# Steps two to four of a four-node LSTM: a second, outer seven-product form around the one in use

## The chip, the core and the metric

The kernel runs on one core of a Trainium2 chip. TensorE (PE) multiplies matrices out of SBUF into PSUM; VectorE (DVE) and ScalarE (ACT) empty PSUM and work element by element; GpSimd (POOL) works on SBUF alone; SyncE (SP) issues the DMAs. The metric is the device time of one launch in microseconds, the median of three runs. Everything is 32-bit float.

## The reference

The kernel computes a stack of four pre-normalised graph layers on x of shape (128, 64, 256), with one 64 by 64 adjacency. What matters here is the end of layer 0 and the start of layer 1:

```python
for p in range(1, MAX_SKIP + 1):                 # MAX_SKIP = 4
    nw = Tv // p
    wins = h[:, :nw * p, :].reshape(Bv * nw, p, Hd)
    last = _lstm_last(Wih[p - 1], Whh[p - 1], bih[p - 1], bhh[p - 1], wins)
    idx = jnp.arange(nw) * p + (p - 1)
    h = h.at[:, idx, :].set(last.reshape(Bv, nw, Hd))

# _lstm_last, one step j of p (zero state at j = 0; i, f, g, o each 256 wide):
g = x_t @ Wih.T + h @ Whh.T + bias
c = sigmoid(f) * c + sigmoid(i) * tanh(gg)
h = sigmoid(o) * tanh(c)

# then: x = x + layer0(...); layer 1 starts with
h = relu(layernorm(x))                           # aggregated by A_hat, then h @ W1.T
```

The change touches p = 4 only, its steps j = 1, 2 and 3, and the hand-over from there to layer 1.

## The kernel before

**Layout.** The nodes' features lie in `hT`, transposed: features on the partitions (two chunks of 128, index c), nodes along the columns. `cols(blk, c, p, j)` picks the columns of node j of each window. For p = 4 there are 512 columns per block, and the blocks form two pairs; the kernel calls a pair with its state `st` (pool `lh0` or `lh1`). It takes the pairs in turn: step 0 of both, step 1 of both, and so on, eight steps in all.

**The seven-product form.** A gate's weight is 256 by 256, so two by two blocks of 128; its data are two feature chunks by two column blocks (a pair). Instead of eight block products, Strassen's scheme in Winograd's variant needs seven, of sums of weight blocks (`S1`, `S2`, `S3`, `S4`, made once per weight on POOL by `weight_sum`, L311) and sums of data blocks (`tx` for the inputs, made on DVE at L650; `th` for the state, made on DVE or POOL in `state_sums`). `gate` (L675) issues these: seven products of the input weight (L688), and for j > 0 seven of the hidden weight (L694) into the same banks a, b and c, 512 columns each. ACT copies (L713) and DVE adds (L710) empty the banks into the gate's tile, and ACT applies bias and sigmoid or tanh (L706). A step without state (j = 0) has three gates and 21 products, one with state four gates and 56.

**After the gates.** `step` (L740) multiplies and adds the cell (L733: on POOL, or on DVE where `both` is given `nc.vector`), ACT takes tanh (L738), and `state` (L653) writes h, or in the last step the result into `hT` (L658), on DVE.

**Order.** The order on each engine's queue is written out by hand: every operation is put into a list by `at(t, ...)` with a virtual time and issued in the order of these times. An engine works off its queue in order, so an operation that waits holds back all behind it. Tiles have fixed places; a new tile in a used place waits for the last reader. PSUM has eight banks of 512 columns, in one pool of eight.

**The weights.** `load` (L791) brings the next p's input weights early and the hidden weights at the start of p (four DMAs of 256 KB each on SP's queue); the sums of the hidden weights follow before step 1. `w1`, layer 1's weight, is loaded at the start of the kernel, and its sums are made in the graph stage (s == 12).

**The hand-over.** While the last LSTM steps run, `begin` (L839) puts layer 1's first tiles between them. For a tile: load x (L572), transpose `hT` back (`turn`, L581, on PE), add it to x (`turned` with direct=True, L587, on DVE from PSUM), statistics (L604, L605) on DVE, the root (L611) on POOL, relu (L616) on ACT, aggregation (`agg`, L625, on PE) and its copy (L629, DVE). `ag_sums` (L837) then prepares the first seven-product form of layer 1, whose products are at L932.

## Time and profile before

| | us |
|---|---|
| median of three runs (lowest, highest) | 1866.76 (1866.54, 1866.87) |
| span of the profiled execution | 1864.5 |
| runs' median less that span | 2.3 |
| busy in the span: PE, DVE, ACT, POOL | 1845.1, 1097.8, 943.3, 816.6 |
| p = 4: about 889 us to the last LSTM product | 1217 |
| layer 1's first product (L932) starts | 1216.99 |

Times inside the kernel are those of one profiled execution, counted from its span's start; the runs are timed from outside, so 2.3 us lie around the span. "Busy" is the time in which an engine had an instruction in work; a matmul's end is modelled by the profile, so two neighbours can overlap in the records, and how far apart they start says more than how long each lasts. A group's row gives the line, the engine, what is written from what, the count, and the mean length in ns.

### The profile page before, as it was taken

To read this page: it belongs to the slowest core of one execution; us is meant where nothing else is said; L and a number is where in the kernel's file an instruction comes from. 1 tells how busy PE (TensorE), PEld (TensorE's weight loads), DVE (VectorE), ACT (ScalarE), POOL (GpSimd) and SP (SyncE) were. 2 spreads that over 40 slices of the span, in tenths; PEclk is the share of its full clock that TensorE was granted. 3 is DMA by queue.
4 is the path that set the end of the run, shared out by engine and by line. 5 is a ranking of instruction groups with operands and counts; after the bars stand their busy time and mean duration, and the time that the engine had idled before them with its cause. 6 is when DMAs were issued, how large, how long until landed. Compare 5 with 4: busy or idle time off the path is not lost.

```text
span 1864.5 us, 21317 instructions
## 1 busy us (share of the span) xinstructions
PE 1845.1 (99%) x7668; PEld 1177.0 (63%) x7668; DVE 1097.8 (59%) x2180; ACT 943.3 (51%) x1622; POOL 816.6 (44%) x773
## 2 busy tenths in 40 slices
PE   8999999999999999999999999999999999999999
PEld 7997444444445666666444444566544899999997
DVE  6775777634546434444633333688876666666664
ACT  6776766534535334433633333477675354444442
POOL 4451423443423533422442222267454566666663
PEclk9999999999999999999999999999999999999999
DMA  5110000000001000000000000333110101111111
GB/s 146 58 58 0 1 1 26 19 1 0 1 0 46 1 0 1 1 1 1 23 0 0 0 0 0 102 113 113 47 47 1 46 12 47 46 46 46 46 46 35
DMA packets 51433, 54.96 MB, mean 29 GB/s; under 512 B 3200, under 2 KB 46720, under 8 KB 51328
## 3 DMA queue, kind: packets, MB, share of 16 engines
q1 hardware_dynamic: 50880, 53.30, 9.1%
q8 instruction: 61, 1.00, 0.2%
q14 instruction: 44, 0.36, 0.1%
q10 hardware_dynamic: 448, 0.30, 0.0%
HBM read 36.55 MB, written 17.04 MB: 29 GB/s over the span
## 4 chain that ended last, share of the span: by engine, by line
PE 93%; DVE 3%; POOL 1%; ACT 1%; issue 1%; DMA 1%; SPq 0%; DVEq 0%; POOLq 0%; ACTq 0%
PE ps L688 34%; PE ps L694 19%; PE ps L1322 8%; PE ps L932 5%; PE ps L1049 4%; PE ps L1409 3%; PE ps L394 3%; PE ps L404 3%; PE ps L1289 2%; PE ps L433 2%; PE ps L1385 2%; PE ps L1419 2%; PE ps L1450 1%; PE ps L625 1%; PE ps L1357 1%; PE ps L581 1%
## 5 line engine op out<-in xcount | busy, mean ns | idle before, releaser
L710 DVE TENSOR_TENSOR gate<-gate,ps 128x512 f32<-128x512 f32 (+2 forms) x378 | 224.0, 620 | 449.1 <-PE ps L694 367.7
L688 PE MATMUL ps<-tx,wih 128*128 128x512 f32 (+2 forms) x996 | 441.3, 541 | 1.9 <-ACT gate L713 1.0
L688 PE MATMUL ps<-hT,wih 128*128 128x512 f32 (+2 forms) x756 | 338.6, 541 | 0.0
L713 ACT COPY gate<-ps 128x512 f32<-128x512 f32 (+2 forms) x252 | 134.3, 533 | 378.6 <-PE ps L694 325.5
L688 PEld LDWEIGHTS ps<-tx,wih 128*128 128x128 f32 x996 | 188.4, 190 | 188.2 <-issue 128.2
L706 ACT ACTIVATE gate<-gate,lbias 128x512 f32<-128x512 f32 (+2 forms) x252 | 216.7, 860 | 160.1 <-DVE gate L710 160.1
L694 PE MATMUL ps<-h,whh 128*128 128x512 f32 (+2 forms) x576 | 256.6, 527 | 0.0
L688 PEld LDWEIGHTS ps<-hT,wih 128*128 128x128 f32 x756 | 143.6, 190 | 141.6 <-issue 79.4
L733 POOL TENSOR_TENSOR gate<-gate 128x1024 f32<-128x1024 f32 (+2 forms) x36 | 71.9, 2019 | 297.6 <-ACT gate L706 297.6
L694 PE MATMUL ps<-th,whh 128*128 128x512 f32 (+2 forms) x432 | 192.4, 527 | 0.0
L694 PEld LDWEIGHTS ps<-h,whh 128*128 128x128 f32 x576 | 109.5, 190 | 100.2 <-issue 76.5
L733 POOL TENSOR_TENSOR cell<-gate 128x1024 f32<-128x1024 f32 (+2 forms) x36 | 79.4, 2230 | 174.8 <-ACT gate L706 174.8
L694 PEld LDWEIGHTS ps<-th,whh 128*128 128x128 f32 x432 | 82.1, 190 | 75.1 <-issue 57.4
L1265 ACT ACTIVATE h<-x,ln_rn 128x256 f32<-128x256 f32 x128 | 68.0, 592 | 92.8 <-POOL ln_rn L1262 92.7
L733 POOL TENSOR_TENSOR cell<-gate,cell 128x1024 f32<-128x1024 f32 (+2 forms) x31 | 62.8, 2044 | 110.2 <-ACT gate L706 110.2
L1322 PE MATMUL ps<-wl,ag 128*128 128x128 f32 x900 | 108.4, 276 | 0.6
L1322 PEld LDWEIGHTS ps<-wl,ag 128*128 128x128 f32 x900 | 104.2, 192 | 3.3 <-ACT ag L1294 2.5
L713 DVE COPY gate<-ps 128x512 f32<-128x512 f32 (+2 forms) x126 | 78.6, 624 | 20.8 <-PE ps L694 20.8
L706 ACT ACTIVATE gate<-ps,lbias 128x512 f32<-128x512 f32 (+2 forms) x126 | 79.5, 631 | 3.8 <-PE ps L694 1.0
L738 ACT ACTIVATE gate<-cell 128x1024 f32<-128x1024 f32 (+2 forms) x72 | 68.0, 951 | 26.1 <-POOL cell L733 26.1
L650 DVE TENSOR_TENSOR tx<-hT,tx 128x512 f32<-128x512 f32 (+2 forms) x70 | 57.7, 824 | 13.8 <-PE ps L688 10.2
L733 POOL TENSOR_TENSOR cell<-cell,gate 128x1024 f32<-128x1024 f32 (+2 forms) x31 | 65.5, 2134 | 0.4
(253 smaller groups left out, 3168.2 us busy)
## 6 DMA issues: line engine op xcount, KB each, us to landing
xt<-in_x_dram SPq DMA_DIRECT2D x30, 512.0 KB, 4.3
x1d<-xt SPq DMA_DIRECT2D x16, 512.0 KB, 2.9
x<-x1d SPq DMA_DIRECT2D x16, 512.0 KB, 4.8
out_dram<-x SPq DMA_DIRECT2D x15, 512.0 KB, 3.8
wih<-in_WihT_dram SPq DMA_DIRECT2D x16, 256.0 KB, 4.9
whh<-in_WhhT_dram SPq DMA_DIRECT2D x12, 256.0 KB, 4.9
xt<-in_x_dram SPq DMA_DIRECT2D x6, 128.0 KB, 2.8
wl<-in_W_dram SPq DMA_DIRECT2D x4, 192.0 KB, 4.0
```

The source lines that it names most:

```text
L650: yield nc.vector.tensor_sub(t[k], *((b[1][0], b[0][0]), (b[1][1], t[0]), (b[1][1], b[1][0]), (b[0][1], t[1 % len(t)]))[k])
L688: nc.tensor.matmul(wide(p_[:, :N]), wih[0][:, OF[k], gi, :], x_, start=first_, stop=(j == 0), skip_group_check=True)
L694: nc.tensor.matmul(p_[:, :N], whh[0][:, OF[k], gi, :], h_, start=False, stop=True, skip_group_check=True)
L706: nc.scalar.activation(to, r[bank_][:, :N] if bank_ else to, fn, bias=lbias[:, l, m : m + 1])
L710: nc.vector.tensor_add(slot(n, hc), slot(n, hc), r[bank_][:, :N])
L713: op(slot(n, hc), r[bank_][:, :N])
L733: fn(*((t["G"] if isinstance(t, dict) and "G" in t else st["c"])[:, n, :, : st["N"]] for t in tiles))
L738: nc.scalar.activation(o_, c, AF.Tanh)
L932: nc.tensor.matmul(r[name], con["w1"][:, OF[j], g, :], x_, start=new, stop=(name, j) in (("a", 4), ("b", 3), ("c", 2)), skip_group_check=True)
L1049: nc.tensor.matmul(banks[name], w2[:, OF[j], k, :], x_, start=(new and k == 0), stop=(k == 1), skip_group_check=True)
L1265: nc.scalar.activation(v[tag][:, q, :], v[src][:, q, :], AF.Relu, bias=v["rn"][:, 1, q : q + 1], scale=v["rn"][:, 0, q : q + 1])
L1322: nc.tensor.matmul(v["g", name][:, p_, :], x_[:, m, ts(p_, P)], wl2[:, OF[j], m, :], start=new and p_ == m == 0, stop=m == 2 and (name, j) ...
```

## The change

For p = 4, steps 1 to 3 no longer call `step` but `outer_step`. A step computes all four gates from x and h together, so its product as a whole has again a two by two shape: rows are the gate pairs (i, g) and (o, f), the inner index is x or h, and columns are the pair's two column blocks. An outer seven-product form goes over these, with weights S1 to S4 (`outer_sum`, on POOL, made once from the input and the hidden weights) and data T1 to T4 (T1 and T3 on DVE, T2 and T4 on POOL). Of its seven outer products, four (5, 2, 4, 3) are computed each by the inner seven-product form, per gate, over two halves of 256 columns (`strassen`, whose data sums are made by `inner_sum` on POOL). Three (1, 6, 7) are computed directly, eight block products of 512 columns each, all into the same four banks k0 to k3 (`direct`). `SEQ` mixes the 28 inner products (each for two gates) and the 24 direct ones evenly. `take` empties an inner bank (ACT copy or DVE add), `chained` a direct one after each of the three products.

The four-node weights are stored in the order i, g, o, f (`load_in_order`, with more and smaller DMAs). Tiles are placed by hand to make room (`outer_places`): the place of `w1` holds some of the sums until the end, so `w1` is loaded in the hand-over and its four sums are made there. PSUM is eight single banks with names, which p = 1 to 3 use in turn (`next_bank`). In step 0 of p = 4 the cell's first products of the second pair go to DVE. In the hand-over `turned` is now an ACT copy, `added` (L593 before, on POOL) adds it to x; the first tile's aggregation is copied by ACT; and the virtual times are others. `fin` marks the last step, which orders some operations differently and splits the last cell operations in two.

```diff
+    def load_w1():
...
-            if s in (9, 12):
+            if s == 9:
                 for k in range(4):
-                    at(1.4 + 1.3 * k, lambda k=k: weight_sum(wih0[0] if s == 9 else con["w1"], k))
+                    at(1.4 + 1.3 * k, lambda k=k: weight_sum(wih0[0], k))
...
-        def turned(self, k, direct=False):
-
-            v, qs = self.v, slice(2 * k, 2 * k + 2)
-            if direct:
-                nc.vector.tensor_add(v["xt"][:, qs], v["xt"][:, qs], v["T", k])
-            else:
-                nc.scalar.copy(v["h"][:, qs], v["T", k])
+        def turned(self, k):
+
+            nc.scalar.copy(self.v["h"][:, slice(2 * k, 2 * k + 2)], self.v["T", k])
...
+    PLACES = ("c", "a0", "b", "k0", "k1", "a1", "k2", "k3")
+    new_banks(**{n: 1 for n in PLACES})
+    turn_ = {"bank": 6, "gate": 0, "a": 0}
+
+    def next_bank():
+        turn_["bank"] += 1
+        return bank(("c", "a0", "k0", "k1", "a1", "b", "k2", "k3")[(turn_["bank"] - 1) % 8])
...
+            due = p == NL and st["pool"] is lh1
             for n in range(2):
-                at(e + 0.1 * n, both(nc.gpsimd.tensor_mul, st, "c", g["i"], g["g"]), n)
+                at(e + 0.1 * n + 0.7 * due, both((nc.vector if due else nc.gpsimd).tensor_mul, st, "c", g["i"], g["g"]), n)
             squash, g["t"] = both(tanh_of, st, g["g"], "c"), g["g"]
             ready = e + 3.5 * u, e + 6.0 * u
-            h_at = t + 13.3
+            h_at = t + (11.5 if p == NL and st["pool"] is lh1 else 13.3)
...
+        if not last and p < NL:
...
+    ORDER = (0, 2, 3, 1)
+    outer = {}
+
+    def load_in_order(src, w):
+        v = src.rearrange("(c p) (g h m) -> h c p g m", p=P, g=4, m=P)
+        for h in range(2):
+            for c in range(2):
+                nc.sync.dma_start(w[:, 2 * h + c, 0:2], v[h, c][:, 0:3:2])
+                for to, g in ((2, 3), (3, 1)):
+                    nc.sync.dma_start(w[:, 2 * h + c, to], v[h, c][:, g])
...
+    def outer_sum(name, engine=nc.gpsimd):
+        x, h, s1, s2, s4 = (outer[n] for n in ("wx", "wh", "s1", "s2", "s4"))
+        M1, M2 = slice(0, 2), slice(2, 4)
+        if name == "S1":
+            engine.tensor_add(s1[:, 0:4], x[:, :, M2], h[:, 0:4, M2])
+        elif name == "S2":
+            engine.tensor_sub(s2, s1[:, 0:4], x[:, :, M1])
+        elif name == "S3":
+            engine.tensor_sub(x[:, :, M2], x[:, :, M1], x[:, :, M2])
+        elif name == "S4":
+            engine.tensor_sub(outer["s4raw"], h[:, 0:4, M1], s2)
+        else:
+            of, k = name
+            w = {"S1": [s1[:, m] for m in range(7)], "H": [h[:, m] for m in range(7)], "S4": s4}[of]
+            op = engine.tensor_sub if k else engine.tensor_add
+            op(*(w[m] for m in ((S1, A21, A22), (S2, S1, A11), (S3, A11, A21), (S4, A12, S2))[k]))
...
+    INNER = (("a", 1), ("c", 2), ("a", 6), ("b", 5), ("a", 7), ("b", 3), ("a", 4))
+    SEQ = sorted([((i + 0.25) * 52 / 28, "S", i) for i in range(28)] +
+                 [((k + 0.5) * 52 / 24, "D", k) for k in range(24)])
+    AT = {(kind, i): n for n, (_, kind, i) in enumerate(SEQ)}
+    CHAIN = ((0, 1), (1, 1), (0, 0), (1, 0))
+    FN = {(0, 0): AF.Sigmoid, (0, 1): AF.Tanh, (1, 0): AF.Sigmoid, (1, 1): AF.Sigmoid}
...
+        def data(pr):
+            v = {5: lambda: T("T1")[:, :, :N], 2: lambda: h(0), 4: lambda: T("T4")[:, :, :N], 3: lambda: h(1)}[pr]()
+            return halves(v), [s[:, :H] for s in T({5: "T1s", 2: "h1s", 4: "T4s", 3: "h2s"}[pr])]
+
+        def inner_sum(pr, k, engine=nc.gpsimd):
+            b, s = data(pr)
+            engine.tensor_sub(*((s[0], b[0, 1], b[0, 0]), (s[1], b[1, 1], s[0]),
+                                (b[0, 1], b[1, 1], b[0, 1]), (s[2], b[1, 0], s[1]))[k])
+
+        def strassen(pr, i):
+            name, k = INNER[i]
+            if i == 0:
+                turn_["a"] ^= 1
+            if (name, k) in (("a", 1), ("b", 5), ("c", 2)):
+                B[pr, name] = bank(f"a{turn_['a']}" if name == "a" else name)
+            b, s = data(pr)
+            d = (b[0, 0], b[1, 0], b[1, 1], s[2], s[0], s[1], b[0, 1])[k - 1]
+            m = OF[k]
+            w = {5: lambda: outer["s1"][:, m], 2: lambda: outer["wh"][:, m, 0:2],
+                 4: lambda: outer["wh"][:, m, 2:4], 3: lambda: outer["s4"][m]}[pr]()
+            for g in range(2):
+                nc.tensor.matmul(B[pr, name][:, g * H : (g + 1) * H], w[:, g, :], d,
+                                 start=(g == 0 and (name, k) in (("a", 1), ("b", 5), ("c", 2))),
+                                 stop=(name, k) in (("a", 4), ("b", 3), ("c", 2)), skip_group_check=True)
...
+        def half(pr, hc, d):
+            return tile_of({5: "22", 2: "11", 4: "21", 3: "12"}[pr])[:, :, hc, d * H : (d + 1) * H]
+
+        def take(pr, i):
+            name, k = INNER[i]
+            hc, d = ((0, 0), (0, 0), (0, 1), (1, 1), (1, 1), (0, 1), (1, 0))[i]
+            v = B[pr, name][:, : 2 * H].rearrange("p (g t) -> p g t", g=2)
+            if pr in (5, 4) and i in (0, 2, 3, 6):
+                nc.scalar.copy(half(pr, hc, d), v)
+            else:
+                nc.vector.tensor_add(half(pr, hc, d), half(pr, hc, d), v)
+
+        def direct(pr, k, c):
+            hc, g = CHAIN[k]
+            if pr == 1 and c == 0:
+                B[k] = bank(f"k{k}")
+            m = 2 * hc + c
+            w = {1: lambda: outer["wx"][:, m, g], 6: lambda: outer["s2"][:, m, g],
+                 7: lambda: outer["wx"][:, m, 2 + g]}[pr]()
+            d = x(0, c) if pr == 1 else T({6: "T2", 7: "T3"}[pr])[:, c, :N]
+            to = wide(B[k][:, :N]) if pr == 1 else B[k][:, :N]
+            nc.tensor.matmul(to, w, d, start=(pr == 1 and c == 0), stop=(c == 1), skip_group_check=True)
...
+        def chained(pr, k):
+            v = B[k][:, :N]
+            if pr == 1:
+                nc.scalar.copy(part("11", k), v)
+            elif pr == 6:
+                nc.vector.tensor_add(part("12", k), part("22", k), v)
+            else:
+                for m in ("21", "22"):
+                    nc.vector.tensor_add(part(m, k), part(m, k), v)
...
+        def in_times_g(n, c=slice(0, KC)):
+            m = ("11", "12")[n]
+            nc.gpsimd.tensor_mul(gate_(m, 0)[:, c], gate_(m, 0)[:, c], gate_(m, 1)[:, c])
+
+        def keep(n):
+            nc.gpsimd.tensor_mul(cell(n), cell(n), gate_(("21", "22")[n], 1))
+
+        def plus(n, c=slice(0, KC)):
+            nc.gpsimd.tensor_add(cell(n)[:, c], cell(n)[:, c], gate_(("11", "12")[n], 0)[:, c])
+
...
+            nc.vector.tensor_mul(h(n), gate_(m, 0), gate_(m, 1))
...
+        def T1(c):
+            nc.vector.tensor_sub(wide(T("T1")[:, c, :N]), x(1, c), x(0, c))
+
+        def T2(engine=nc.gpsimd):
+            engine.tensor_sub(T("T2")[:, :, :N], h(1), T("T1")[:, :, :N])
+
+        def T3(c):
...
+            nc.vector.tensor_sub(wide(T("T3")[:, c, :N]), wide(h(1)[:, c]), x(1, c))
+
+        def T4():
+            nc.gpsimd.tensor_sub(T("T4")[:, :, :N], h(0), T("T2")[:, :, :N])
...
+            prep(-38 + 0.6 * c, T1, c, needs_h=False)
+        for k, s in ((0, -35), (1, -34), (3, -33)):
+            prep(s, inner_sum, 5, k, needs_h=False)
+        for k, s in ((0, -25), (1, -24), (3, -23)):
+            prep(s, inner_sum, 2, k)
+        prep(-15, T2)
+        prep(-14.9, inner_sum, 5, 2)
+        late = 8 if one else -11
+        prep(late, T4)
+        prep(late + 0.1, inner_sum, 2, 2)
+        for k in range(4):
+            prep(late + 2 + k, inner_sum, 4, k)
+        late = 18 if fin else 1
+        for c in range(KC):
+            prep(late + 0.6 * c, T3, c)
+        for k in range(4):
+            prep(late + 6 + k, inner_sum, 3, k)
+
+        for n, (_, kind, i) in enumerate(SEQ):
+            if kind == "S":
+                mi, i = divmod(i, 7)
+                tick(n, strassen, (5, 2, 4, 3)[mi], i)
+                tick(n + 1.1, take, (5, 2, 4, 3)[mi], i)
+            else:
+                di, i = divmod(i, 8)
+                tick(n, direct, (1, 6, 7)[di], *divmod(i, 2))
+                if i % 2:
+                    tick(n + 1.15, chained, (1, 6, 7)[di], i // 2)
...
+        e = AT["D", 19] + 4.2
+        for n in range(2):
+            tick(e + 0.2 * n, keep, n)
+        tick(e + 0.1, plus, 0)
+        tick(54.6, squash, 0)
+        for i, (g, hc) in enumerate(((0, 0), (1, 0), (0, 1), (1, 1))):
+            tick((51.3, 53.5)[hc] + 0.1 * g if fin else (58.2, 61.2)[hc] + 1.2 * g, act, "12", g, hc)
+        e = 56.2 if fin else 63
+        for c in range(KC if fin else 1):
+            c = slice(c, c + 1) if fin else slice(0, KC)
+            tick(e, in_times_g, 1, c)
+            tick(e, plus, 1, c)
+        tick(58.5, out, 0)
+        tick(e + 4.2, squash, 1)
+        tick(e + 6, out, 1)
+        st["h_at"] = t0 + 0.5 * (e + 6)
+        return t0 + 26
...
+        elif p > 1:
+            at(t + 7.5, outer_places, l)
+            for when, name in ((16, "S1"), (18.8, "S2"), (21.6, ("S1", 0)), (23.5, ("S1", 1)), (24.5, ("S1", 2)),
+                               (25.5, ("S1", 3)), (27, ("H", 0)), (28.5, ("H", 1)), (30, ("H", 3)),
+                               (48.2, "S4"), (48.3, ("H", 2)), (50, "S3"), (52, ("S4", 0)), (52.5, ("S4", 1)),
+                               (53, ("S4", 2)), (53.5, ("S4", 3))):
+                at(t + when, outer_sum, name)
...
-                    if p == NL and turn:
-                        turn = None if st is sts[-1] else False
+                    if p == NL and j:
+                        if j == 1 and st is sts[0]:
+                            t += 3
+                            n = turn_["gate"] - 1
+                            tags = {"22": (n + 1) % 5, "11": (n + 2) % 5, "12": (n - 2) % 5,
+                                    "21": (n - 1) % 5, "spare": n % 5}
+                        else:
+                            tags = dict(tags)
+                            tags["22"], tags["spare"] = tags["spare"], tags["22"]
+                        t = outer_step(t, st, j, j == p - 1, l, tags, j == p - 1 and st is sts[-1])
+                        continue
                     t = step(t, st, j, j == p - 1, l, wt[l], turn)
...
-    t -= 28
+    t -= 26
+    seam = []
+
+    def seam_bank():
+        if not seam:
+            return bank(f"a{1 - turn_['a']}")
+        seam.append(seam.pop(0))
+        return bank(seam[-1])
...
+        def turned(k):
+            f.turn(k)
+            f.turned(k)
+
+        def added(k):
+            f.added(k)
+            if k:
+                f.store()
+
+        def agg(c):
+            f.agg(c)
+            f.agged(c, nc.vector.tensor_copy if s else nc.scalar.copy)
...
+    at(t + 7.6, make_room)
+    begin(0, 7.7, 11.4, 12.5, 16.3, 23.2)
+    begin(1, 7.8, 16, 17.1, 21.1, 28)
+    begin(2, 7.9, 20.3, 21.4, 25.3)
+    begin(3, 17, 24.3, 25.4)
+    begin(4, 21.4)
+    at(t + 17.3, load_w1)
     for k in range(4):
-        at(t + 35.3 + 0.1 * k, ag_sums, 0, k, nc.vector)
+        at(t + 24 + 0.1 * k, lambda k=k: weight_sum(con["w1"], k))
+    at(t + 26.1, lambda: seam.extend(("a0", "a1", "c", "b")))
+    at(t + 34, lambda: First(3).root())
+    for k in range(4):
+        at(t + 28.7 + 0.1 * k, ag_sums, 0, k, nc.vector)
```

## The prediction

> **What bounds the kernel now.** I read the page's busy table and its chain first.
>
> ```profile
> PE 1845.1 (99%) x7668; PEld 1177.0 (63%) x7668; DVE 1097.8 (59%) x2180; ACT 943.3 (51%) x1622; POOL 816.6 (44%) x773
> ...
> PE 93%; DVE 3%; POOL 1%; ACT 1%; issue 1%; DMA 1%; SPq 0%; DVEq 0%; POOLq 0%; ACTq 0%
> PE ps L688 34%; PE ps L694 19%; PE ps L1322 8%; PE ps L932 5%; PE ps L1049 4%; PE ps L1409 3%; PE ps L394 3%; PE ps L404 3%; PE ps L1289 2%; PE ps L433 2%; PE ps L1385 2%; PE ps L1419 2%; PE ps L1450 1%; PE ps L625 1%; PE ps L1357 1%; PE ps L581 1%
> ```
>
> TensorE (PE) is busy 99% and carries 93% of the chain; the LSTM products (L688, L694) alone are 53% of it. So every product that is removed shortens the kernel, unless an engine that was hidden becomes late. Next, busy time by window (columns: window, its length, then busy time and instructions of PE, weight loads, VectorE (DVE), ScalarE (ACT), GpSimd (POOL), granted clock, DMA share, GB/s): the layer-4 LSTM's stretch, two of its steps, and the hand-over to layer 1.
>
> ```profile
> 921.00:1210.00 289.00, 289.00 (x710) 130.94 (x709) 122.24 (x195) 104.37 (x144) 92.46 (x48) 1.00 0.05 17
> 1105.00:1153.00 48.00, 48.00 (x113) 21.28 (x112) 18.65 (x26) 16.51 (x22) 13.93 (x6) 1.00 0.00 0
> 1153.00:1201.00 48.00, 48.00 (x131) 22.73 (x130) 24.04 (x52) 19.48 (x29) 15.84 (x10) 1.00 0.21 69
> 1201.00:1229.00 28.00, 27.66 (x118) 16.30 (x117) 23.30 (x49) 16.39 (x26) 12.41 (x9) 1.00 0.32 100
> ```
>
> PE never pauses from 921 to 1210 us, at full granted clock, and loses 0.34 us in the hand-over. DVE, ACT and POOL have more than half of each step free. That slack is what the change spends.
>
> **The products.** The timeline on PE, a step of 512-column products and a run of 256-column ones (start, time, line, shape, count):
>
> ```profile
> 1105.09 1.02 PE L688 MATMUL ps<-tx,wih 128*128 128x512 f32 x2
> 1105.95 1.02 PE L694 MATMUL ps<-th,whh 128*128 128x512 f32 x2
> ...
> 69.03 3.62 PE L404 MATMUL ps<-wg,g 128*128 128x256 f32 x16
> ```
>
> A product leaves two records, and the next product starts 0.86 us later (1105.95 − 1105.09), 0.859 as a mean over many. For 256 columns, 16 records take 3.62 us; the last lasts about 0.38 (the group's mean is 380 ns), so they start (3.62 − 0.38)/15 = 0.216 us apart, and a product takes 0.431 us. A step at j = 1, 2 or 3 has 4 gates × 7 × 2 = 56 products, 48.1 us (the 48 us windows hold 113 records). In the changed kernel it has four outer products, each 7 inner ones × 2 gates of 256 columns, 56 × 0.431 = 24.2 us, and three direct ones of 8 products each, 24 × 0.859 = 20.6 us: 44.8 us. Six steps: 6 × (48.1 − 44.8) = **−19.9 us**.
>
> [...]
>
> **What feeds them.** DVE per step: 20 inner adds and 12 chained ones out of PSUM (L710's row: 684 ns), 21.9 us, and T1, T3 and the two outputs, about 5 us: 27 of 44.8. ACT: 12 copies (584 ns), 16 activations (722) and 2 tanh (1,048): 20.7. POOL: 16 sums of 256 columns (L425's row: 729 ns), 11.7 us, and eight 1024-column ones (T2, T4, two each of i·g, keep and plus; 2,351 ns), 18.8: 30.5 of 44.8, where before had 13.9 to 15.8 of 48. None exceeds PE, so load alone costs nothing; order can. Two things bring order in. One is the place where DVE and POOL hold each other up (timeline):
>
> ```profile
> 576.97 1.22 DVE L733 TENSOR_TENSOR cell<-gate,cell 128x1024 f32<-128x1024 f32 x1 [1.70 <-ACT gate L706]
> 578.30 3.19 DVE L733 TENSOR_TENSOR cell<-cell,gate 128x1024 f32<-128x1024 f32 x1
> ...
> 577.79 2.62 POOL L733 TENSOR_TENSOR cell<-gate,cell 128x1024 f32<-128x1024 f32 x1 [7.36 <-ACT gate L706]
> ```
>
> The second DVE instruction, of the same size, starts while POOL runs one, and takes 3.19 instead of 1.22 us. DVE's add out of PSUM at 581.41 keeps to 0.68 while POOL is busy. So T1, T3 and the outputs (two SBUF inputs) can each lose up to one POOL instruction, 2.35 us, and the 32 adds can't. [...]
>
> The other is the queue behind the output. Output 1 waits on DVE for tanh 1 (ACT), which waits for POOL's i·g 1 and plus 1; behind it on DVE stands the add that empties the bank of inner product S2.2, needed again two inner products later. Counting from the order, DVE has only 0.2 to 0.3 us to spare there. Bounds: 0 (a step of before loses nothing) to 2.35 (one POOL instruction); I take 0.3 in five of six steps, **+1.5 us**, nearer to zero because the adds themselves aren't slowed.
>
> **The transition from j = 0.** The weights' outer sums (S1 to S4 of 1024 columns, and twelve inner ones of 256 or 512) now follow on POOL, behind the hidden weights' load (issued at 889, in 12 DMAs instead of 4; landing rows: 4.9 us each) and beside DVE's input differences. Most have more than 5 us of room. Bounds 0 to 5 us (two POOL instructions); I take **+1.0**, near the low end, as 921 to 1210 shows no wait behind the sums made today. SP's queue holds nothing else in that stretch that anyone awaits soon.
>
> **The hand-over to layer 1.** Before, DVE added PSUM to x (L587). Now ACT copies and POOL adds (L593's row: 1,275 ns), the four sums of w1 (4 × 0.73 = 2.9 us; they leave the graph stage, where POOL is busy 4 to 5 tenths and PE 9, so nothing is gained there) lie on POOL here, and its banks are rotated, some reused at once. The row that prices a reuse:
>
> ```profile
> 1213.75 0.69 DVE L629 COPY ag<-ps 128x512 f32<-128x512 f32 x1 [0.20 <-PE ps L625]
> ...
> 1215.09 0.37 PEld L688 LDWEIGHTS ps<-tx,wih 128*128 128x128 f32 x2 [0.49 <-DVE gate L710]
> 1215.27 1.02 PE L688 MATMUL ps<-tx,wih 128*128 128x512 f32 x2
> ```
>
> PE to evictor 0.20, ACT copy 0.58, release to the next product 0.23 (L710 ends at 1215.04): 1.0 us. In the order:
> (i) the third tile's turn is followed directly by S3.0 on the same bank, and the fourth's by the first aggregation: 2 × 1.0, a third place 0.3: 2.3 us.
> (ii) The second tile's aggregation waits for DVE's last inner add, queued behind the fourth tile's statistics, which wait for POOL's add behind keep, plus, keep (3 × 2.35): 1.7 to 2.5.
> (iii) The third tile's aggregation waits for a DVE copy queued behind statistics that wait for POOL's add behind w1's sums (2.9): 1.8 to 2.0.
> (iv) A layer-1 product waits for an ACT eviction behind the last tanh, which waits for POOL's halves of i·g and plus (4 × 1.275): 2.7 to 6.5.
> (ii) and (iii) hold PE back 3.5 us, which (iv)'s chain uses: it keeps 0 to 3.0, taken as 1.5. With the low ends of (ii) and (iii), as these chains start from products further ahead than I can place exactly: 2.3 + 1.7 + 1.8 + 1.5 = **+7.3 us**. Bounds: 0, as in before's hand-over (0.34), and 13.3, all four at their tops.
>
> Layers 1 to 3 and the LSTMs of one to three nodes get the same instructions with the same dependencies (eight single banks take turns where one pool of eight did): 0, between −1 and +1 (PE's idle time there is about 2 us).
>
> **Sum** against the profiled execution: 1864.5 − 19.9 + 1.5 + 1.0 + 7.3 = 1854.4 us of span; 2.3 us lie around the span (median 1866.76), so **1856.7 us**.
>
> **The rivals.** All hidden (0.14): the terms given back stay near zero, as the idle halves of the three engines would have it: 1864.5 − 19.9 + 0 to 3 + 2.3 = 1847 to 1850. Against it stand the direct bank reuses (i), which no slack removes.
> Given back in full (0.10): the hand-over at its top (13.3), the steps at 0.7 each: 1864.5 − 19.9 + 13.3 + 4.2 + 2.5 + 2.3 = 1867: no change. For it: DVE is busy about 45 of 52 us there.
> POOL becomes the bound (0.12), on the slower side: with 30.5 of 44.8 us and a recurrence that passes POOL five times per step (i·g, keep, plus, T2 or T4, inner sums), a late output makes the next step's sums late, so slack isn't regained. It decides from (19.9 − 8.3)/6 = 1.9 us of stall per step; with one and a half POOL instructions (3.5 us) per step the time is 1866.8 + 6 × 3.5 − 19.9 + 8.3 = 1876. Against it: a POOL instruction's whole length, 2.35, would have to show in each step, and POOL has 14 us of idle time to catch up in.
> The smaller products aren't half as long (0.01): were the 56 further loads per step (190 ns each) to lie bare, 6 × 56 × 0.190 = 64 us, 1921 us; L404's row is against it.
> My forecast, part of it given back mainly at the hand-over, has 0.63: 1850.5 to 1863.
>
> A difference of 0.2%, 3.7 us, is about what can be told from no change here. Faster by more: 0.63 + 0.14 + part of the third = 0.78; within: 0.09; slower: 0.13. The range leaves out the lowest few hundredths and POOL's case: 1848 to 1867.
>
> **What would show it.** Right: PE's 256-column records 0.216 us apart, a step of about 45 us, PE waits of 5 to 9 us around the turns (L588), aggregation (L626) and the first layer-1 products (L1265), under 0.5 us per step elsewhere. Wrong: waits of 2 us or more in every step for POOL's or DVE's sums, or no waits at the hand-over at all.

## The result, and the profile after

The changed kernel takes 1864.36 us (median of 20 runs, 1861.67 to 1866.61); the kernel before took 1866.91 beside it (20 runs, 1866.25 to 1867.52). The ratio is 0.9987, with an interval of 0.9980 to 0.9994: faster by 2.5 us, an eighth of the 19.9 us of products that were removed. The forecast was 1856.7, so 7.7 us more came back than was forecast. Two things in the numbers ask for an answer: where the rest went, and why runs of the changed kernel differ by 5 us among themselves where those of before differ by 1.3.

The page after, busy times and chain:

```profile
PE 1832.1 (98%) x7956; PEld 1234.1 (66%) x7956; DVE 1162.3 (62%) x2250; ACT 964.1 (52%) x1680; POOL 949.1 (51%) x895
...
PE 92%; POOL 2%; DVE 2%; ACT 2%; issue 1%; DMA 1%; SPq 0%; POOLq 0%; DVEq 0%; ACTq 0%
```

PE is still the bound, but its busy time fell by 13.0 us only (1845.1 to 1832.1), not 19.9: some of the remaining products got longer. The windows say where. Columns are as in the prediction; the granted clock is the third number from the end. First the transition out of step 0 in the kernel before, which the prediction did not look at by itself:

```profile
898.00:945.00 47.00, 47.00 (x110) 20.72 (x109) 29.42 (x36) 24.89 (x34) 25.39 (x16) 1.00 0.00 0
```

and in the kernel after, that stretch, two whole outer steps, and pieces of the slow stretches:

```profile
898.00:945.00 47.00, 42.19 (x110) 21.57 (x109) 35.47 (x38) 23.40 (x34) 46.45 (x34) 0.93 0.00 0
1005.00:1050.00 45.00, 45.00 (x162) 30.55 (x161) 29.07 (x38) 18.96 (x30) 33.93 (x25) 1.00 0.00 1
1050.00:1095.00 45.00, 45.00 (x162) 30.46 (x161) 29.29 (x39) 18.96 (x30) 33.94 (x25) 1.00 0.00 1
...
912.00:915.00 3.00, 3.00 (x5) 1.23 (x4) 1.98 (x3) 0.72 (x1) 2.92 (x4) 0.50 0.00 0
936.00:939.00 3.00, 2.81 (x5) 1.60 (x6) 0.00 (x0) 1.08 (x2) 3.00 (x3) 0.50 0.00 0
1220.00:1222.00 2.00, 2.00 (x6) 0.97 (x5) 1.16 (x2) 1.64 (x4) 1.92 (x3) 0.50 0.00 0
```

The outer steps themselves run as forecast: PE is busy without a gap, at full clock. In the transition POOL is busy 46.45 of 47 us, PE 42.19, and the granted clock is 0.50 in two places; once more in the hand-over. The timeline on PE, with the waits in brackets, shows what precedes each of the three:

```profile
911.00 2.80 PE L701 MATMUL ps<-tx,wih 128*128 128x512 f32 x4 [2.26 <-ACT gate L726]
936.18 2.07 PE L965 MATMUL ps<-hT,wih 128*128 128x512 f32 x2 [2.54 <-ACT gate L719]
974.83 1.03 PE L940 MATMUL ps<-early 128*128 128x256 f32 x4
1019.60 1.03 PE L940 MATMUL ps<-early 128*128 128x256 f32 x4
1190.58 1.13 PE L940 MATMUL ps<-h,wih 128*128 128x256 f32 x4 [0.68 <-ACT h L588]
1199.30 1.16 PE L626 MATMUL ps<-ahT,h 128*128 128x128 f32 x8 [0.67 <-ACT ag L588]
1207.46 2.05 PE L626 MATMUL ps<-ahT,h 128*128 128x128 f32 x16 [1.25 <-DVE gate L954]
1212.78 1.13 PE L626 MATMUL ps<-ahT,h 128*128 128x128 f32 x8 [1.55 <-DVE ag L630]
1217.93 1.10 PE L1265 MATMUL ps<-T,w 128*128 128x512 f32 x2 [3.16 <-ACT hS L1270]
```

Two waits in the transition, none between 940 and 1190, five in the hand-over. A whole step lasts 1019.60 − 974.83 = 44.77 us. Each of the three longest waits is followed by half the clock: the products from 911.00 to 917.06 are five, 4.3 us at full clock, and took 6.06, which is 1.8 lost; in the same way 1.6 at 936.18 and 1.7 from 1218.87 on. The account for the profiled execution:

| | forecast, us | found, us |
|---|---|---|
| products removed | −19.9 | −19.9 (6 × (48.1 − 44.77) = −20.0) |
| waits in the steps | +1.5 | 0 |
| waits in the transition | +1.0 | 2.26 + 2.54 = +4.8 |
| waits in the hand-over | +7.3 | 0.68 + 0.67 + 1.25 + 1.55 + 3.16 = +7.3 |
| half clock after three waits | none | 1.8 + 1.6 + 1.7 = +5.1 |
| wait of before that is gone | none | −0.3 |
| sum | −10.1 | −3.0 |

The spans differ by 1863.0 − 1864.5 = −1.5. All of that arises in the stretch of the change: ahead of it the two timelines lie 0.05 us apart (the same product starts at 879.73 before and 879.78 after), and from the turn at 1230.77 before and 1229.22 after they keep a distance of 1.5 to 1.6 us to the end, so the LSTMs of one to three nodes and the layers behind the hand-over gave nothing back. Of the 1.5 us left over in the account, restarts are about 0.5 (the first product after a wait takes about 0.95 us to the next instead of 0.86, at five places in the hand-over); the rest isn't resolved.

### The profile page after: what moved, and what is told of

It is laid out like the page before. It is cut to its first block, busy times and chain, and to the rows that moved or that the text cites. A ratio compares the mean times of both kernels' runs of the same rounds, so it can differ in the third digit from the quotient of the medians.

```text
span 1863.0 us, 22263 instructions
## 1 busy us (share of the span) xinstructions
PE 1832.1 (98%) x7956; PEld 1234.1 (66%) x7956; DVE 1162.3 (62%) x2250; ACT 964.1 (52%) x1680; POOL 949.1 (51%) x895
## 4 chain that ended last, share of the span: by engine, by line
PE 92%; POOL 2%; DVE 2%; ACT 2%; issue 1%; DMA 1%; SPq 0%; POOLq 0%; DVEq 0%; ACTq 0%
PE ps L701 26%; PE ps L707 12%; PE ps L1655 8%; PE ps L940 7%; PE ps L965 6%; PE ps L1265 5%; PE ps L1382 4%; PE ps L396 3%; PE ps L406 3%; PE ps L1742 3%; PE ps L1622 2%; PE ps L435 2%; PE ps L1718 2%; PE ps L1752 2%; PE ps L1783 1%; PE ps L626 1%
## 5 line engine op out<-in xcount | busy, mean ns | idle before, releaser
L723 DVE TENSOR_TENSOR gate<-gate,ps 128x512 f32<-128x512 f32 (+2 forms) x306 | 176.6, 604 | 303.1 <-PE ps L707 227.6
L701 PE MATMUL ps<-tx,wih 128*128 128x512 f32 (+2 forms) x804 | 344.2, 530 | 4.2 <-ACT gate L726 3.3
L701 PE MATMUL ps<-hT,wih 128*128 128x512 f32 (+2 forms) x612 | 265.9, 530 | 0.0
L719 ACT ACTIVATE gate<-gate,lbias 128x512 f32<-128x512 f32 (+2 forms) x204 | 171.7, 842 | 117.1 <-DVE gate L723 117.0
L707 PE MATMUL ps<-h,whh 128*128 128x512 f32 (+2 forms) x384 | 158.6, 494 | 0.0
L755 POOL TENSOR_TENSOR gate<-gate 128x1024 f32<-128x1024 f32 (+2 forms) x24 | 43.9, 1851 | 181.8 <-ACT gate L719 181.8
L954 DVE TENSOR_TENSOR gate<-gate,ps 128x512 f32<-128x512 f32 x120 | 82.0, 683 | 69.4 <-PE ps L940 67.0
L707 PE MATMUL ps<-th,whh 128*128 128x512 f32 (+2 forms) x288 | 118.9, 494 | 0.0
L985 ACT ACTIVATE gate<-gate,lbias 128x512 f32<-128x512 f32 x96 | 64.9, 717 | 57.4 <-DVE gate L954 30.3
L755 POOL TENSOR_TENSOR cell<-gate,cell 128x640 f32<-128x640 f32 (+2 forms) x20 | 37.2, 1874 | 67.4 <-ACT gate L719 67.4
L1742 PE MATMUL ps<-wvo,h3T 128*128 128x256 f32 x256 | 65.5, 379 | 0.0
```

Of the source, the lines that this page charges most:

```text
L701: nc.tensor.matmul(wide(p_[:, :N]), wih_of(l, k, gi), x_, start=first_, stop=(j == 0), skip_group_check=True)
L707: nc.tensor.matmul(p_[:, :N], whh[0][:, OF[k], gi, :], h_, start=False, stop=True, skip_group_check=True)
L719: nc.scalar.activation(to, r[bank_][:, :N] if bank_ else to, fn, bias=lbias[:, l, m : m + 1])
L723: nc.vector.tensor_add(slot(n, hc), slot(n, hc), r[bank_][:, :N])
L755: fn(*((t["G"] if isinstance(t, dict) and "G" in t else st["c"])[:, n, :, : st["N"]] for t in tiles))
L954: nc.vector.tensor_add(half(pr, hc, d), half(pr, hc, d), v)
```

## The experiments

All runs change the kernel after, but for the two with pauses, which change the kernel before. Waits are PE's in the profiled execution of each, between 905 and 945 (transition) and 1185 and 1225 (hand-over). The last column is the time lost to half clock there: the granted clock's distance from 1.00, times the window, summed over windows of 0.5 us.

| run | median (range), us | span, us | waits in transition | waits in hand-over | lost to half clock |
|---|---|---|---|---|---|
| kernel after | 1864.36 (1861.67–1866.61) | 1863.0 | 2.26, 2.54 | 7.3 | 5.1 |
| e1_cells_first | 1868.84 (1863.50–1869.54) | 1867.1 | 3.02, 3.25 | as after | 8.5 |
| e2_dma_order | 1864.08 (1861.74–1866.54) | 1863.2 | 1.39, 3.66 | as after | 5.1 |
| e3_t3_late | 1861.46 (1859.54–1862.85) | 1860.5 | 2.51, 1.41 | as after | 3.4 |
| e4_cells_first_t3_late | 1862.18 (1860.89–1862.94) | 1860.6 | 3.01, 1.06 | as after | 3.4 |
| e5_t1_late | 1865.93 (1860.78–1867.23) | 1864.5 | 0.45, 0.86, 3.44 | 7.3 | 6.8 |
| e6_t1_t3_late | 1860.55 (1859.93–1861.58) | 1858.3 | 0.47, 0.82, 1.41 | 7.3 | 1.7 |
| e7_seam | 1862.11 (1861.70–1863.04) | 1860.4 | 2.29, 3.92 | 0.69, 2.71, 1.24 | 3.4 |
| e8_all | 1857.23 (1856.80–1859.41) | 1855.1 | 0.44, 0.84, 1.41 | 0.69, 2.71, 1.24 | 1.7 |
| e11_best | 1856.83 (1856.34–1859.06) | 1856.5 | 0.45, 0.82, 0.42 | 0.69, 2.72, 2.68 | 1.7 |
| e12_pool_load | 1856.73 (1856.36–1857.94) | 1854.6 | 0.45, 0.84, 0.41 | 0.69, 2.69, 1.50 | 1.7 |

The waits and the half clock are nearly all that sets these versions apart: the span less both lies between 1845.0 and 1847.0 us in all eleven, while the spans run from 1854.6 to 1867.1.

**Is POOL late with the cells, or are the weights?** e1_cells_first:

```diff
...
-(16, "S1"), (18.8, "S2"), (21.6, ("S1", 0)), (23.5, ("S1", 1))
+(16, "S1"), (22.5, "S2"), (22.4, ("S1", 0)), (23.5, ("S1", 1))
...
```

> The two cell products of step 0 (L755) go ahead of the second outer weight sum and one inner sum on POOL's queue. Theory (order): the first wait of PE in the transition (2.3 us before 911.0) comes from those sums standing ahead of the cells, which holds up tanh on ACT and behind it the copy that empties a bank; and the halved clock after it (912 to 915.5, about 1.7 us) comes from the pause. Then both go: 1864.4 - 2.3 - 1.7 = 1860.4 us, and the granted clock has one dip less. Rival (load): POOL is busy 47.6 of 48 us from 897 to 945, so what is moved behind is late instead; a wait of about 2 us turns up before 945 and the time stays within 1 us of 1864.4. Rival (loads of weights): the twelve smaller DMAs land too late; the order changes nothing, 1864.4.

My first theory fell. The cells ran first, tanh and the copy were in time, and PE waited longer:

```profile
911.91 2.96 PE L701 MATMUL ps<-tx,wih 128*128 128x512 f32 x4 [3.02 <-DVE tx L662]
```

None of the three times expected was met: the median is 4.5 us above the kernel after. In the profiled executions (1867.1 against 1863.0) the waits are 1.5 us longer and the half clock, which lasted about 6.8 us after two of the three long waits instead of 3.4, costs 3.4 more. The first wait is now put down to DVE's input difference L662. In the kernel after, both ended within 0.15 us of each other, and the profile had named the later one, ACT. The timeline on DVE of the kernel after shows why L662 is late:

```profile
906.02 3.69 DVE L1017 TENSOR_TENSOR early<-hT,hT 128x512 f32<-128x512 f32 x2
909.64 1.22 DVE L662 TENSOR_TENSOR tx<-hT 128x512 f32<-128x512 f32 x1
...
928.28 3.92 DVE L1027 TENSOR_TENSOR T<-h,hT 128x512 f32<-128x512 f32 x2
932.13 0.67 DVE L954 TENSOR_TENSOR gate<-gate,ps 128x512 f32<-128x512 f32 x1
932.73 0.67 DVE L723 TENSOR_TENSOR gate<-gate,ps 128x512 f32<-128x512 f32 x1
```

T1 (L1017) stands ahead of L662, and T3 (L1027) ahead of the last add of step 0 (L723). Both read two SBUF inputs while POOL works without a pause, and take 3.7 and 3.9 us for two instructions (T1 0.93 and 2.84, T3 2.25 and 1.75); the adds out of PSUM beside them keep to 0.67. The same T3 in the last outer step, where POOL runs nothing from 1167.91 to 1173.36, takes 0.69:

```profile
1170.37 0.69 DVE L1027 TENSOR_TENSOR gate<-h,hT 128x512 f32<-128x512 f32 x1
```

That POOL is what stretches them is read from these rows; no run takes POOL's work away from beside T1 and T3. e2_dma_order issues first all the DMAs that the first sum needs:

```diff
-        load_in_order(a["WhhT"][l], outer["wh"])
...
+        for m in range(4):
+            for to, g in ((2, 3), (3, 1)):
+                nc.sync.dma_start(w[:, m, to], v[m // 2, m % 2][:, g])
+        for m in range(4):
+            nc.sync.dma_start(w[:, m, 0:2], v[m // 2, m % 2][:, 0:3:2])
```

> The eight DMAs of the hidden weights that the first outer sum reads are issued first, the four others behind them; nothing else. POOL's first sum started at 897.66, when the last of twelve had landed; it should start about 4 x 0.55 = 2.2 us earlier, at 895.5. Theory (order on POOL): the sums ahead of the cells are then done by 902.0 and the cells start at 902.4 as in the kernel before, so the first wait (2.3) and its slow clock (1.7) go: 1860.4 us. Rival (load): POOL gains 2.2 us, so the wait shrinks but what follows stays saturated: 1862 to 1864. If the dominant cause is DVE and POOL holding each other up rather than POOL's lateness: 1864, the wait stays.

POOL's first sum did start at 895.34 and the cells at 902.61, as expected; yet the first wait only shrank to 1.39, the second grew to 3.66, and the time stayed. So late weights had a share in the first wait, but earlier weights alone buy nothing.

**T3 and T1 behind what a bank waits for.** e3_t3_late, and e5_t1_late:

```diff
-            prep(late + 0.6 * c, T3, c)
+            prep((6 if one else late) + 0.6 * c, T3, c)
```

> In the first outer step T3's two subtractions on DVE (928.28, 3.92 us instead of 1.4) go behind the next inner add and the last add of step 0 (L723). Theory (order, with POOL blocking DVE): the second wait (2.5 us before 936.18) goes, as the add runs at 928.3 instead of 932.7, and with it the slow clock behind it (1.7): 1864.4 - 4.2 = 1860.2 us. Rival (load): another operation waits for POOL's sum in its place, PE still pauses 2 us or more between 930 and 945: 1864. Rival (no clock effect, the records only show it): 1861.9.

```diff
-            prep(-38 + 0.6 * c, T1, c, needs_h=False)
-        for k, s in ((0, -35), (1, -34), (3, -33)):
+            prep((-33 if one else -38) + 0.6 * c, T1, c, needs_h=False)
+        for k, s in ((0, -32), (1, -31), (3, -30)) if one else ((0, -35), (1, -34), (3, -33)):
```

> Only the first outer step's T1 (two DVE subtractions) and the three inner sums on POOL that follow from it are put behind the two input differences (L662) of step 0 that the second pair's third gate needs. The run with the cells first showed that the first wait of PE stays (3.0 us, now put down to DVE's L662). Theory (DVE's order with POOL blocking it): T1, slowed from 1.4 to 3.7 us by POOL, stands ahead of L662; now L662 ends near 908 and the wait before 911 shrinks from 2.3 to at most 0.7 us (what ACT's copy leaves), its slow clock goes; the second wait (2.5) remains: 1864.4 - 1.6 - 1.7 = 1861.1 us. Rival (POOL's lateness alone, through tanh and ACT's copy): the wait stays at 2.3 us, 1864.

PE's waits in the transition, first in e3, then in e5 (timeline on PE), and the windows of e3's transition and of the stretch around e5's long wait:

```profile
911.41 1.96 PE L701 MATMUL ps<-tx,wih 128*128 128x512 f32 x4 [2.51 <-DVE tx L662]
934.15 1.13 PE L965 MATMUL ps<-hT,wih 128*128 128x512 f32 x2 [1.41 <-ACT gate L719]
...
912.57 1.12 PE L701 MATMUL ps<-tx,wih 128*128 128x512 f32 x2 [0.45 <-DVE gate L723]
927.72 1.12 PE L701 MATMUL ps<-tx,wih 128*128 128x512 f32 x2 [0.86 <-DVE gate L723]
935.02 2.08 PE L965 MATMUL ps<-hT,wih 128*128 128x512 f32 x2 [3.44 <-ACT gate L719]
```

```profile
898.00:945.00 47.00, 43.08 (x122) 22.58 (x121) 39.57 (x42) 23.79 (x34) 46.37 (x31) 1.00 0.00 0
...
934.00:940.00 6.00, 4.98 (x10) 3.33 (x11) 1.77 (x3) 1.91 (x3) 6.00 (x6) 0.50 0.00 0
```

e3 took the second wait from 2.54 to 1.41 and gained 2.9 us; forecast were 4.2, as the wait was to go entirely. Its time is near the 1861.9 of the rival without a clock effect, but not for that reason: in its profiled execution the waits are 0.9 us less and the half clock cost 1.7 us less. The wait of 2.51 that stayed was not followed by half clock this time, and the one of 3.17 in the hand-over was, for 6.7 us. e5 took the first wait from 2.26 to 0.45 as the theory had it, but PE then came earlier to the second place, where it waited 3.44 instead of 2.54, and in six of eleven runs the mean clock was 0.996: 1865.93, with single runs down to 1860.78, at a mean clock of 1.000. The profiled execution shows why the median rose: its waits add up to as much as those of the kernel after (12.1 us), and the half clock lasted 6.8 us after each of the two long ones, so it cost 6.8 us instead of 5.1. e4 adds the cells' order to e3:

> Both reorderings (cells first on POOL, T3 later on DVE). Theory (order): both waits and both dips of the clock go, 1864.4 - 4.0 - 4.2 = 1856.2 us. Rival (load): POOL's saturated 48 us remain, PE comes to each place 4 us earlier and meets waits of 2 to 4 us there: 1860 to 1863. Rival (no clock effect): 1864.4 - 4.8 = 1859.6.

It is no better than e3 (1862.18 against 1861.46): POOL's order ahead of the cells was not the cause by itself. e6 has T1 and T3 late:

> T1 and T3 of the first outer step both later. Theory: both waits of the transition shrink to under 1.5 us together and no dip of the clock is left there: 1864.4 - 3.5 - 3.4 = 1857.5 us. Rival (POOL's load): POOL is as full as before, so PE meets its sums late further on; a new wait of 2 us or more between 915 and 945, 1860 to 1862.

```profile
912.72 1.12 PE L701 MATMUL ps<-tx,wih 128*128 128x512 f32 x2 [0.47 <-DVE gate L723]
927.84 1.12 PE L701 MATMUL ps<-tx,wih 128*128 128x512 f32 x2 [0.82 <-DVE gate L723]
933.10 1.13 PE L965 MATMUL ps<-hT,wih 128*128 128x512 f32 x2 [1.41 <-ACT gate L719]
```

1860.55: three waits of 2.7 us in all, no slow clock in the transition of its profiled execution. 3.8 us gained, where 6.9 were expected: of the 4.8 us of waits 2.1 went, and 2.7, behind DVE and ACT, are left. The time lies in the range of the rival (1860 to 1862), but the new wait of 2 us or more that it named is not in the trace: POOL is no less full than before (busy 54.06 of the 55 us from 905 to 960, in the kernel after 50.30), and the waits did not come back in full elsewhere. No run takes POOL's own work out of the transition, so what that load costs apart from the order stays open.

**The hand-over.** e7_seam puts the fourth tile's statistics behind the rest, gives the last halves of the cell (`in_times_g` and `plus`) to DVE, and moves a turn and an aggregation by one product:

```diff
-            nc.gpsimd.tensor_mul(gate_(m, 0)[:, c], gate_(m, 0)[:, c], gate_(m, 1)[:, c])
+            (nc.vector if fin and n else nc.gpsimd).tensor_mul(gate_(m, 0)[:, c], gate_(m, 0)[:, c], gate_(m, 1)[:, c])
...
-            nc.gpsimd.tensor_add(cell(n)[:, c], cell(n)[:, c], gate_(("11", "12")[n], 0)[:, c])
+            (nc.vector if fin and n else nc.gpsimd).tensor_add(cell(n)[:, c], cell(n)[:, c], gate_(("11", "12")[n], 0)[:, c])
...
-        e = 56.2 if fin else 63
+        e = 56.6 if fin else 63
...
-(t_turn and t_turn - 1.2, turned, 0)
+(t_turn and t_turn - (1.7 if s == 2 else 1.2), turned, 0)
...
-    begin(0, 7.7, 11.4, 12.5, 16.3, 23.2)
+    begin(0, 7.7, 11.4, 12.5, 16.3, 23.6)
...
-    begin(3, 17, 24.3, 25.4)
+    begin(3, 17, 24.3, 31.5)
```

> Only the hand-over is changed: the fourth tile's statistics go behind everything else on DVE, the last cell's halves (L995, L1001) go from POOL to DVE, and the third tile's first turn and the first aggregation each move by one product, so that no bank is reused at once. Theory (the five waits of 7.3 us there are the order on DVE, POOL and the banks, as the prediction had it): bank reuse 1.35 to 0.3, the aggregations' 1.2 and 1.5 to 0.3 or less, and the layer-1 wait 3.2 to about 2; then 4 to 5 us of waits go, and the slow clock behind the long one (2 us) if it falls under 2 us: 1864.4 - 4.5 = 1860, or 1858. Rival (DVE's load, 45 of 52 us busy): the waits come back on DVE, 1863 to 1865.

```profile
1203.03 1.10 PE L940 MATMUL ps<-gate,wih 128*128 128x256 f32 x4 [0.69 <-DVE gate L954]
1212.98 3.18 PE L1265 MATMUL ps<-T,w 128*128 128x512 f32 x4 [2.71 <-DVE T L1166]
1222.21 1.12 PE L1265 MATMUL ps<-T,w 128*128 128x512 f32 x2 [1.24 <-DVE hS L1273]
```

The waits for a bank and for the aggregations are gone (i to iii of the prediction); in place of the 7.3 us stand 4.64, now behind DVE, which carries the halves. 1862.11: 2.3 us gained, about half of the 4.5 expected; the rival, that waits come back on DVE, is right in part. e8_all joins e6 and e7:

> The two changes of the transition and those of the hand-over together. Theory: the gains add, 1857.5 - 4.5 to 6.5 = 1851 to 1853 us, below the kernel before by 14. If the halved clock depends on where the pause falls in time rather than on its length, the sum can miss by 2 us either way. Rival (load): 1858 or more.

1857.23, ratio to the kernel before 0.9953 (0.9941 to 0.9966). The parts add, and a little more (3.8 + 2.3 against 7.1 found). It missed the expected 1851 to 1853 by 4.2 to 6.2 us, which is what e6 (3.1) and e7 (2.1) missed of theirs together.

**What a wait costs beyond its length.** Two kernels stop PE in the kernel before on purpose, inside the four-node steps:

```diff
+    def pause(n):
+        p_ = bank()
+        nc.tensor.matmul(p_[:, :8], ident, mhalf, start=True, stop=True)
+        nc.vector.tensor_copy(scr, p_[:, :8])
+        for _ in range(n):
+            nc.vector.tensor_scalar_mul(scr, scr, 1.0)
+        nc.tensor.matmul(p_[:, 8:16], ident, scr, start=True, stop=True)
...
+                    if p == NL and j and 2 * (j - 1) + (st is sts[1]) in (0, 1, 2, 3):
+                        at(t + 10.5, pause, 4)
```

The last two lines are those of e9_short_pauses; e10_long_pauses has `in (0, 2)` and `pause, 12`.

> The kernel before with PE stopped four times in its four-node steps (in steps 1 and 2 of both pairs): a tiny product, a DVE copy of it and four tiny DVE instructions on it, then a tiny product of that. Four pauses of about 1.0 us each (0.2 to DVE, five instructions of some 0.12 us, 0.2 back). Theory (only a long pause lowers the clock): the granted clock stays at 1.00 and the time grows by the pauses alone, 1866.7 + 4 x 1.1 = 1871. Rival (every pause lowers it): four dips, 1871 + 4 x 1.7 = 1878. Rival (the clock has its own rhythm and no link with pauses): dips in both this and the next kernel, or in neither.

> The kernel before with two pauses of PE, the same way but with twelve tiny instructions, about 2.2 to 2.8 us each. Theory (a pause over some 2 us halves the granted clock for about 3.4 us, which costs another 1.7): 1866.7 + 2 x 2.6 + 2 x 1.7 = 1875, with up to 3.4 us of spread from run to run as the same pause sometimes goes without a dip (runs of one kernel had mean clocks of 0.995 to 0.999). Rival (no clock effect): 1866.7 + 5.2 = 1872 and the clock at 1.00.

The four short pauses were 1.08 us each. Time 1874.10 (1874.05 to 1874.85), so 1.78 us per pause, the mean clock 1.000 in every run, and a spread of 0.8 us. The expected 1871 had left out the tiny products: from the first of them to the next full product a pause takes 1.61 us (936.09 to 937.70), and 0.08 more at the restart, which makes 6.8 of the 7.1 us found. The two long ones, in one execution (timeline on PE; then windows):

```profile
939.43 0.39 PE L803 MATMUL ps<-scr_p,ident 128*128 128x8 f32 x2 [2.73 <-DVE scr_p L802]
1040.62 0.39 PE L803 MATMUL ps<-scr_p,ident 128*128 128x8 f32 x2 [2.74 <-DVE scr_p L802]
```

```profile
939.00:942.00 3.00, 2.56 (x6) 1.30 (x7) 0.94 (x3) 0.00 (x0) 0.00 (x0) 0.70 0.00 0
942.00:945.00 3.00, 3.00 (x7) 1.25 (x6) 2.01 (x3) 0.00 (x0) 0.00 (x0) 0.73 0.00 0
...
1040.00:1043.00 3.00, 2.38 (x7) 1.28 (x8) 2.43 (x7) 0.00 (x0) 0.00 (x0) 1.00 0.00 0
1043.00:1046.00 3.00, 3.00 (x8) 1.33 (x7) 1.15 (x2) 1.42 (x2) 0.00 (x0) 1.00 0.00 0
```

Two pauses of the same length: after the first the clock falls, after the second it doesn't. The runs of this kernel lie between 1875.96 and 1880.74 (median 1877.86), with mean clocks of 0.999 to 0.996. With its tiny products a long pause takes 3.26 us (936.42, where the first tiny product starts, to 939.68, the next full one) and 0.08 at the restart, so without any fall the time would be 1866.98 + 2 × 3.34 = 1873.7; the runs lie 2.3 to 7.0 above, that is 1.1 to 3.5 us for each pause. So a pause of 1.1 us costs its length, and one of 2.7 us costs its length and an uncertain 0 to 3.5 us.

The profiles of all these runs show how uncertain. In the windows a stretch of half clock lasts 3.4 us, which costs 1.7, or 6.7 to 6.8 us, which costs 3.4 (e5's around 935 above). Of the waits in the table and the deliberate pauses, each of the 13 of 3.01 us or more was followed by one, six of them by the long kind. Of the 11 between 2.26 and 2.74 us seven were, all of the short kind; none of 1.56 us or less was. In e11_best a wait of 2.72 us was not followed by half clock and one of 2.68 us, nine us later, was. The slowest run of e10, 7.0 us above, is what two long stretches would cost (6.8). That would also explain the spread in the kernel after: its runs at a mean clock of 0.999 lie between 1861.67 and 1864.09, those at 0.997 between 1864.63 and 1866.61, and its range of 4.9 us is about three short stretches. What decides between no half clock, 3.4 us of it and 6.7 to 6.8 us isn't shown by any run.

**The best version, and the margin in the steps.** e11_best adds to e8 two moves in the transition:

```diff
-        at(t0 + 14.2, act, 0, 1, "a")
+        at(t0 + (13.1 if l == NL - 1 and gi == 3 and st["pool"] is lh1 else 14.2), act, 0, 1, "a")
...
-                at(e + 0.1 * n + 0.7 * due, both((nc.vector if due else nc.gpsimd).tensor_mul, st, "c", g["i"], g["g"]), n)
+                at(e + 0.1 * n + (0.7 + 1.4 * n) * due, both((nc.vector if due else nc.gpsimd).tensor_mul, st, "c", g["i"], g["g"]), n)
```

> The version with the transition and the hand-over reordered, and two more moves in the transition: the second cell product of the second pair's step 0 on DVE goes behind the add that a bank waits for (0.84 us wait before 927.6), and the activation that frees a bank for the direct products goes ahead of a longer one on ACT (1.41 us before 932.8). Theory (order): 1857.2 - 0.84 - 1.41 = 1855.0 us. Rival (POOL's load decides there): the waits move on by some microseconds and the time stays at 1857.

1856.83 (ratio 0.9949, 0.9936 to 0.9961): the waits in the transition are down to 1.69, by 1.0 instead of 2.25, as one of 0.42 for POOL's sum and one of 0.82 for a DVE add took their place; no difference from e8 can be told. It is faster than both kernels, by 10.1 us than before. e12_pool_load loads POOL further in the four outer steps between the first and the last:

```diff
+        if not one and not fin:
...
+                nc.gpsimd.tensor_mul(C["more"][:, n, :, :N], cell(n), cell(n))
```

> The reordered version (1856.8 us) with two further POOL products of 1024 columns (2.35 us each, squares of the cell that nobody reads) in the four outer steps between the first and the last, so that POOL is busy 35 of 45 us there. Theory (the outer steps have slack, the loss lies at their two ends): PE still waits for nothing in the four steps, or under 0.5 us in each; 1857 to 1859. Rival (the steps run close to POOL's bound and are bare of waits by a hair): each step is held up by one POOL instruction, 2 us or more, and with the slow clock 1865 or more.

1856.73, and PE's steps don't move (window of one step):

```profile
1005.00:1050.00 45.00, 45.00 (x162) 30.60 (x162) 29.29 (x39) 19.20 (x31) 37.67 (x27) 1.00 0.00 1
```

POOL is busy 37.67 of 45 us instead of 33.9 (the two squares take 3.75 us together, not the 4.7 expected) and PE still waits for nothing. POOL's work in the steps is not the bound, with at least 3.7 us per step to spare; how much more it could carry isn't shown.

## Why the prediction was wrong

The forecast failed at the transition from j = 0, and in having no term for the half clock behind a long wait. Its own sign for being right, PE waits under 0.5 us outside the hand-over, fails at two places of the transition and nowhere else; neither of its signs for being wrong came up.

- **Products: right.** A step is 44.77 us against 44.8 forecast; the records of 256 columns stayed at half of those of 512 (four from 963.63 to 964.50, two of 512 from 962.77 to 963.63), and the loads stayed hidden, as in L404's row: PE was busy 45.00 of 45 us beside 161 loads of 30.55 us in all. No run shows the term of the rival with 1921 us, 56 further loads per step lying bare: PE's records rose by 288 in six steps, so there are 48 per step, none of them bare. (At 190 ns each, the mean of before's load rows L688 and L694, bare ones would have been 55 us, not 64.)
- **The steps: right in kind, too careful.** The 0.3 us per step were 0. The rival with POOL as the bound needed 1.9 us of stall per step and is excluded by the kernel after itself, whose steps have none. POOL has 11 us of idle time per step (45 less 33.9, a little more work than the 30.5 forecast), and e12 shows that PE waits for nothing with 3.7 us less of it either.
- **The transition: the step that failed.** The prediction put +1.0 there for the sums of the weights, "near the low end, as 921 to 1210 shows no wait behind the sums made today", with a top of 5. It was 4.8 of waits, just inside that top, and 3.4 of half clock. The window of the reason given starts at 921, after the first of the two waits. The load of POOL was added up for a whole outer step (30.5 of 44.8) and not for the transition, where step 0's cells, the weights' sums and the data sums of the first outer step meet: 46.45 of 47 us, against 25.39 before. And what DVE and POOL cost each other was priced at the outputs of the steps, where it cost nothing, and not at T1 and T3 of the first outer step, where two instructions took 3.7 and 3.9 us instead of 1.4 and stood ahead of what two banks waited for. e3, e5 and e6 show these two places by moving T1 and T3; e1, e2 and e4 show that neither the cells' place nor the late weights were the cause by themselves, though both looked so in the profile. That POOL's fullness, and not only the order, holds the engines up there is argued from the windows; it wasn't tested.
- **The hand-over: the sum right, its parts less so.** (i) 1.35 for 2.3, (ii) 1.25 for 1.7, (iii) 1.55 for 1.8, (iv) 3.16 for 1.5. The mechanisms were those named, as the timelines of the kernel after show for (ii), on DVE, and (iv), on ACT:

```profile
1206.19 0.43 DVE L603 BATCH_NORM_STATS2 ln_st<-xt 128x6 f32<-128x256 f32 x1 [1.97 <-POOL xt L592]
...
1216.20 1.06 ACT L1004 ACTIVATE gate<-cell 128x1024 f32<-128x1024 f32 x1 [3.88 <-POOL cell L1001]
```

(iv) came out above the 0 to 3.0 that was given for it: POOL's halves took 5.85 us (1.28, 1.27, 1.71 and 1.59) instead of 4 × 1.275, and (ii) and (iii) covered 2.8 us of the chain instead of 3.5. e7 removed three of the four. That the sum agrees to a tenth is luck, as four errors of 0.25 to 1.7 us cancel. DVE, "busy about 45 of 52 us" in the rival that gives all back, was busy 38.6 (1173 to 1225).

- **The clock: a missing term.** No line of the sum had it, since before's granted clock was 1.00 throughout; a trace whose waits on PE, behind the first product, are 0.9 us or less can't show what a long wait costs. It was 5.1 us in the profiled execution, and e9 and e10 price it apart from anything else. With it, the transition's true waits and no waits in the steps, the forecast span of 1854.4 becomes 1854.4 + 3.8 + 5.1 − 1.5 = 1861.8, against 1863.0 measured. (A timed run of either kernel lies 1.7 to 1.8 us above its own span; the 2.3 of the prediction holds 0.6 by which the profiled execution of before was quicker than the median.)
- **The rivals.** The result lies between the forecast's own band, which ends at 1863, and the 1867 of "given back in full", but it did not take that rival's way: the hand-over stayed at 7.3, far from 13.3, and the steps at 0.

## What to carry to other kernels

Add up each engine's load for every stretch between two regimes, not for the steady step alone: what was idle on average can be full for 47 us, and there an order that was harmless decides. In a kernel like this one, price a new wait of PE between products of 2.26 us or more at its length and 0, 1.7 or 3.4 us more (in these runs never 0 from 3.01 us on), one of 1.56 us or less at its length and 0.1, and break a long one into shorter ones if it can't be removed: four pauses of 1.08 us left the mean clock at 1.000, two of 2.73 and 2.74 us brought it to 0.996 to 0.999. When two releasers of a wait end close together, 0.15 us apart in the kernel after, the profile names the later one only, and to take that one away may change nothing, as in e1: look first at what else ended just before.

## What the runs showed of the hardware

A pause of PE of 2.73 us was followed by half the granted clock for 3.4 us, and one of 2.74 us in the same execution was not; four of 1.08 us never were. Over the waits and pauses of all profiles above, each of 13 from 3.01 to 3.92 us was followed by half the granted clock for 3.4 or 6.7 to 6.8 us, seven of 11 between 2.26 and 2.74 us for 3.4 us, and none of 1.56 us or less. VectorE subtractions of 512 columns with two SBUF inputs took 0.93 and 2.84 us (T1) and 2.25 and 1.75 us (T3) beside a busy GpSimd, instead of the 0.69 of the same T3 in the last step, where GpSimd was idle, and GpSimd's own sums stretched too (S4 3.34 us instead of 2.35), while adds out of PSUM kept to 0.67.
